# Two layers of decomposed-position attention: low-rank factors and key places loaded behind x

## The chip, the cores and the metric

The kernel runs on one core of one Trainium2 chip. The metric is the device time of one execution in microseconds (us); lower is better. The core's engines each work through an instruction stream of their own: TensorE (PE, with its weight loads shown as PEld), VectorE (DVE), ScalarE (ACT), GpSimd (POOL) and SyncE (SP). Transfers that SP issues run on the queue that the profile calls q1, those that POOL issues on q0; both are carried out by the same 16 DMA engines.

## The reference

x has 48 x 48 positions of 768 channels. Two layers follow each other, each adding attention of its normalised input to that input. Cut to what matters:

```python
def _gn(v, G=32, eps=1e-5):            # 32 groups of 24 channels, over all positions
    m, s = mean(v by group), var(v by group)
    return (v - m) / sqrt(s + eps)

# layer 0, low-rank addition to q and v
qkv = x @ qkv_w + qkv_b
u = x @ FacTu_w                        # 768 -> 16
qkv[..., :C]  += u @ q_facts_w @ FacTv_w
qkv[..., 2*C:] += u @ v_facts_w @ FacTv_w
# both layers, 12 heads of 64
attn = softmax((q * scale) @ k.T + rel_h + rel_w)   # rel_h, rel_w from q and tables
out = attn @ v @ proj_w + proj_b

x = x + layer0(_gn(x))
x = x + layer1(_gn(x))
```

## The kernel before

All of x fits on the chip. It is handled in six blocks of 384 tokens (`NQB`, `QB`). Layer 0 begins with `load_transposed`: SP issues the six loads of x (1152 KB each), then the first third of the weights of k (`weights.load(0)`, 768 KB, tile `w_k`). `weights.begin` then issues the small loads of layer 0. TensorE turns each block with 18 transposes into PSUM (tiles `psx`), ACT copies the result out (`raw`, six copies for a block), and DVE takes statistics of each copy (`stats`, L187).

`group_norm` follows. DVE aggregates the statistics (`mv`, L204), TensorE sums them over the channels of a group (`sum_mean`, L210) and spreads the mean back (`bc_mean`), then the same for the variance (`sum_var`, `bc_rstd`). With mean and deviation DVE normalises the blocks (L249), and the products of k begin (`ps_k`, L523), then those of v, then those of q; the seven products of a two-by-two block scheme replace eight. Attention, the output projection and layer 1 come after that.

The low-rank part of layer 0 is not computed on x. `fold` adds FacTu @ facts @ FacTv to the weights of v and q, when those are read, with products of the tiles `low` and `fv`. To make `low`, the generator `low_rank` turns FacTu (tile `fu`) with six TensorE transposes (`psu`), DVE copies them (`fuT`, two copies), and four products with the small matrices (tile `facts`, made wider by three POOL copies, L321) give `psl`, which ACT copies into `low`. The generator stops before its first product; each `next` on it runs it on to the next stop. Two of its products stand before `sum_mean` on TensorE, the others between the steps of `group_norm`.

Three other things stand on POOL at the start. It builds two one-hot tables, stores them (`f_hot`, L143) and loads them back four times as `places` (L154), which the scores of attention read. `weights.spread` copies the position tables from `flat` into `tab` (L311, four copies), which the products of q's positions read. And it stores the six raw blocks as residuals (`f_res`, L192, 1152 KB each), which the output projection of layer 0 reads.

Each engine runs its own stream in the order in which a scheduler set it when the kernel was built; `in_order` marks instructions for that scheduler. [...] The scheduler's order of the kernel before is, on POOL: f_hot, fu, f_hot, four fv and two facts loads, places, the facts copies, the table copies, the six f_res stores. On SP: x, `w_k`, bt, v_bias, four flat loads, the second third of `w_k`.

A second copy of the whole computation stands in the program under a branch for results that fail a test of range (`shifted`); it isn't executed here.

Of the kernel before, what the change touches and what calls it, by code (L numbers as in the profile page):

```python
# [18 lines left out]
P = 128  # L19
# [15 lines left out]
RANK = 16  # L35
# [36 lines left out]
def compute(ctx: ExitStack, tc: tile.TileContext, x, layers, out, run, bad):  # L72


    nc = tc.nc
    shifted = bad is None
# [53 lines left out]
    with ExitStack() as hots:  # L130
# [4 lines left out]
        for i, (rows, pattern, shape) in enumerate(parts):  # L135
            t = hotp.tile([rows, *shape], F32, tag=f"h{i}", name=f"hot_{i}")
# [15 lines left out]
    def load_places():  # L152
        for i in range(4):
            nc.gpsimd.dma_start(  # L154
                places[ts(i, 2 * KG)].bitcast(F32), hot.rearrange("k (u n) -> k u n", u=2)
            )

    def in_order(instruction):

        tc.keep_in_program_order(instruction)  # L160
# [4 lines left out]
    def load_transposed(xT, raw, res, weights, low_rank):  # L165


        with tc.tile_pool(name="ps_x", bufs=3, space=PSUM) as ps_x:
            loaded = [xT[b].rearrange("p t q -> p (t q)") for b in range(NQB)]
            loaded = [l.rearrange("p (j c) -> p j c", j=TPB) for l in loaded]  # L170
            for b in range(NQB):
                nc.sync.dma_start(loaded[b], x[ts(b, QB), :].rearrange("(j p) c -> p j c", p=P))
            weights.load(0)
            weights.begin()
            if not shifted:
                load_places()
            for b in range(NQB):
                if b == 2:
                    next(low_rank)
                for t in range(CT):  # L180
                    ps = ps_x.tile([P, QB], F32, tag="ps", name=f"psx_{b}_{t}")
                    for j in range(TPB):
                        in_order(nc.tensor.transpose(
                            ps[:, ts(j, P)], loaded[b][:, j, ts(t, P)], ident
                        ))
                    nc.scalar.copy(raw[b][:, t, :], ps)
                    nc.vector.bn_stats(stats[:, t, b, :], raw[b][:, t, :])  # L187

            weights.spread()
            for b in range(HB):  # L190
                for i in (b, b + HB):
                    in_order(nc.gpsimd.dma_start(res[i], raw[i]))  # L192
# [63 lines left out]
    class Weights:  # L256
# [20 lines left out]
        def begin(self):  # L277
            one, ly = self.one, self.ly
            if ly.lora is not None:
                u_w, q_f, v_f, o_w = ly.lora  # L280
                self.fu = one.tile([P, CT, RANK], F32, tag="fu", name="fu")
                nc.gpsimd.dma_start(self.fu, u_w.rearrange("(t p) r -> p t r", p=P))
                self.facts = one.tile([RANK, 2, P], F32, tag="facts", name="facts")
                nc.gpsimd.memset(self.facts, 0.0)
                self.out = one.tile([P, C], F32, tag="fv", name="fv")
                self.low = one.tile([P, 2, C], F32, tag="low", name="low")
                for i, f in enumerate((q_f, v_f)):
                    nc.gpsimd.dma_start(self.facts[:, i, 0:RANK], f)
                for r in range(4):
                    nc.gpsimd.dma_start(self.out[r * 32 : r * 32 + RANK, :], o_w)  # L290
            self.bt = one.tile([P, 3 * CT], F32, tag="bt", name="bt")
            nc.sync.dma_start(self.bt, ly.qkv_bt)
            nc.sync.dma_start(v_bias[self.li], ly.qkv_bt[:, 2 * CT :])

            self.tables = []
            for a, src in enumerate((ly.relh_t, ly.relw_t)):
                flat = one.tile([P, REL], F32, tag=f"flat{a}", name=f"flat{a}")
                tab = one.tile([P, REL, 2], F32, tag=f"tab{a}", name=f"tab{a}")  # L300
                nc.gpsimd.memset(tab, 0.0)
                for par in range(2):
                    nc.sync.dma_start(flat[ts(par, HD), :], src)
                self.tables.append((flat, tab))
# [954 lines left out]

    es = ExitStack()  # L1260
    xT, gn, weights = begin(0, es)
    for li, ly in enumerate(layers):
        last = li == len(layers) - 1
        with tc.tile_pool(name="p1_kv", bufs=1, **REUSE) as kv:
            raw = xT
            low_rank = weights.low_rank(kv)
            if li == 0:


                raw = [  # L1270
                    kv.tile([P, 2, CT, QB], F32, tag=tag, name=f"raw_{tag}")
                    for tag in ("t1", "t2", "vw")
                ]
                raw = [raw[b % HB][:, b // HB] for b in range(NQB)]
                load_transposed(xT, raw, residuals[0], weights, low_rank)
                first, k_steps = third_of_k(weights, 0)
            normalise = group_norm(xT, raw, gn, low_rank, k_steps)
            qd, kd, vd, rel_d = project(ly, li, xT, kv, weights, first, normalise)
# [5 lines left out]
        with tc.tile_pool(name="p3_w", bufs=1, **REUSE) as p3:  # L1284
# [22 lines left out]
            if last:  # L1307
                p3_first = es.enter_context(
                    tc.tile_pool(name="p3_first", bufs=1, side="right", **REUSE)
                )  # L1310

                y_2, y_1, *first_out, y_0 = (
                    p3_first.tile(shape, F32, tag=name, name=name)
                    for name, shape in (
                        ("y_1_2", [P, 2, C]), ("y_1_1", [P, 2, C]), ("oT_1_0", [P, CT, QB]),
                        ("oT_1_1", [P, CT, QB]), ("y_1_0", [P, 2, C]),
                    )
                )
                first_out += [y_0, y_1, y_2]
            else:  # L1320
                xT, gn, weights = begin(1, es)
                first_out = [xT[HB], xT[NQB - 1]]
# [73 lines left out]
```

## Time and profile before

| | us |
|---|---|
| median of 3 runs | 3257.7 (3254.74 to 3259.03) |
| profiled execution, its own time | 3255.04 |
| its span, first to last instruction | 3253.3 |
| TensorE busy | 3204.2 (98%) |
| first transpose of block 0 | 6.28 |
| first transpose of block 5 | 24.32 |
| group sums of the mean (sum_mean) | 29.14 |
| first product of k | 36.37 |
| first scores of attention | about 507 |

The profile is one execution; its times count from the first instruction of the span. In the timeline a row has the start and the length of a run of equal instructions, the engine, the line, the operation with its tiles, the count, and in brackets how long the engine stood idle before and what ended that. The length of a DMA row is the time its issue took at the issuer, not that of the transfer.

### The profile page before, as it was taken

Reading aid. Unit: us, or ns where it says so; the run is one execution under the profiler, and the core shown is the slowest. Engines: PE = TensorE matmul, PEld = TensorE weight load, DVE = VectorE, ACT = ScalarE, POOL = GpSimd, SP = SyncE. Lnnn points to the kernel's source line nnn. Section 1 sums busy time; section 2 is a strip of 40 time slices with the busy share of each in tenths; the row PEclk is TensorE's granted clock in tenths of the full one; section 3 lists DMA queues with packets and bytes.
Section 4 is the critical chain, followed back from the end, with each engine's and each line's share of the span. In section 5 each row is a group of like instructions: output and inputs, shape, how many; then the busy total and the mean of one; then the engine's idle time right before and its main releaser. Section 6 shows DMA issues by size and latency. Waiting matters only on the chain.

```text
span 3253.3 us, 50008 instructions
## 1 busy us (share of the span) xinstructions
PE 3204.2 (98%) x19600; PEld 1990.3 (61%) x19600; DVE 2112.3 (65%) x2281; ACT 1450.7 (45%) x1673; POOL 470.1 (14%) x855
## 2 busy tenths in 40 slices
PE   8999999999999999999989999999999999999999
PEld 5555666665666565666555566666566565656565
DVE  8532437777777777777775234577777777777764
ACT  3111436555555565553012024556556566555520
POOL 2145110000000000000012541102202221100000
PEclk9999999999999999999999999999999999999999
DMA  7333388353526263634234335765636473735351
GB/s 264 130 88 74 128 257 219 84 127 79 138 68 153 64 156 65 142 75 151 112 117 141 68 100 183 244 151 135 124 109 156 106 167 81 164 76 132 70 203 60
DMA packets 225155, 419.76 MB, mean 129 GB/s; under 512 B 43616, under 2 KB 111104, under 8 KB 221072
## 3 DMA queue, kind: packets, MB, share of 16 engines
q1 hardware_dynamic: 177712, 255.35, 31.9%
q0 software_dynamic: 47200, 161.12, 16.3%
q8 instruction: 158, 2.59, 0.3%
q14 instruction: 85, 0.70, 0.1%
HBM read 260.35 MB, written 155.97 MB: 128 GB/s over the span
## 4 chain that ended last, share of the span: by engine, by line
PE 81%; issue 12%; POOL 2%; DMA 2%; DVE 1%; SPq 1%; ACT 1%; POOLq 0%; DVEq 0%; ACTq 0%
PE ps_sc L954 34%; PE ps_ov L954 25%; PE ps_v L523 7%; PE ps_q L698 4%; PE ps_k L523 4%; PE psy L1186 4%; PE ps_d L954 1%; PE psr L637 1%; DMA f_r<-relw 1%; POOL f_k L567 1%; POOL f_q L630 1%; DMA flat<-in_relh_t_dram 0%; POOL f_r L663 0%; PE psc L637 0%; ACT pt L981 0%
## 5 line engine op out<-in xcount | busy, mean ns | idle before, releaser
L987 DVE TENSOR_TENSOR sum<-sum,pt 128x1024 f32<-128x1024 f32 (+1 forms) x960 | 1071.1, 1116 | 185.7 <-ACT pt L981 95.5
L981 ACT ACTIVATE pt<-ps_sc 128x1024 f32<-128x1024 f32 (+1 forms) x1080 | 1010.4, 941 | 168.9 <-PE ps_sc L954 84.0
L954 PE MATMUL ps_sc<-q,k 64*128 64x512 f32 (+1 forms) x8640 | 1082.2, 370 | 1.6 <-DVE relw L392 0.7
L954 PEld LDWEIGHTS ps_sc<-q,k 64*128 64x128 f32 x8640 | 778.9, 185 | 213.8 <-issue 45.6
L954 PE MATMUL ps_ov<-pt,v 128*64 128x512 f32 (+1 forms) x4320 | 857.7, 551 | 0.0
L954 PEld LDWEIGHTS ps_ov<-pt,v 128*64 128x64 f32 x4320 | 301.1, 137 | 497.6 <-issue 443.0
L954 PE MATMUL ps_sc<-rel,places 64*128 64x512 f32 (+1 forms) x2160 | 411.9, 370 | 1.4 <-DMA rel<-f_r 1.4
L698 PE MATMUL ps_q<-xT,w_q 128*128 128x384 f32 x864 | 285.3, 488 | 0.7 <-DVE v L587 0.7
L1032 POOL DMA_DIRECT2D f_rec<-rec x120 | 58.8, 494 | 1570.6 <-DVE rec L1021 1569.0
L1026 ACT ACTIVATE o<-o,v_bias 128x512 f32<-128x512 f32 (+1 forms) x60 | 40.9, 682 | 451.4 <-DVE o L1025 451.4
L698 PEld LDWEIGHTS ps_q<-xT,w_q 128*128 128x128 f32 x864 | 163.1, 191 | 110.3 <-issue 2.6
L954 PEld LDWEIGHTS ps_sc<-rel,places 64*128 64x128 f32 x2160 | 210.4, 185 | 32.8 <-issue 2.2
L1021 DVE RECIPROCAL rec<-ps_d 128x512 f32<-128x512 f32 (+1 forms) x60 | 181.9, 3031 | 2.5 <-PE ps_d L954 2.5
L601 POOL DMA_DIRECT2D f_v<-v x288 | 137.9, 488 | 105.8 <-DVE v L587 100.9
L987 DVE TENSOR_TENSOR sum<-pt 128x1024 f32<-128x1024 f32 (+1 forms) x60 | 67.0, 1116 | 124.3 <-ACT pt L981 124.3
L704 DVE TENSOR_SCALAR x_q<-ps_q,bt 128x384 f32<-128x384 f32 x72 | 44.3, 617 | 158.8 <-PE ps_q L698 158.8
L523 PE MATMUL ps_k<-xt,w_k 128*128 128x384 f32 x432 | 143.4, 487 | 3.6 <-DVE xt L427 2.6
L996 ACT CAST sum<-sum 128x1024 bf16<-128x1024 f32 (+1 forms) x60 | 57.7, 961 | 168.4 <-DVE sum L987 168.4
L523 PE MATMUL ps_k<-xT,w_k 128*128 128x384 f32 x324 | 115.4, 510 | 4.7 <-DVE xT L249 4.6
L523 PEld LDWEIGHTS ps_k<-xt,w_k 128*128 128x128 f32 x432 | 81.5, 190 | 63.0 <-PE ps_k L523 3.0
L999 DVE TENSOR_TENSOR sum<-sum,sum 128x1024 bf16<-128x1024 f32 (+1 forms) x60 | 67.1, 1119 | 61.6 <-ACT sum L998 61.6
L997 DVE TENSOR_TENSOR sum<-sum,sum 128x1024 f32<-128x1024 f32 (+1 forms) x60 | 67.1, 1119 | 61.6 <-ACT sum L996 61.6
(183 smaller groups left out, 2474.0 us busy)
## 6 DMA issues: line engine op xcount, KB each, us to landing
rel<-f_r SPq DMA_DIRECT2D x1152, 96.0 KB, 4.3
f_k<-xs POOLq DMA_DIRECT2D x72, 384.0 KB, 2.9
f_q<-xs_q POOLq DMA_DIRECT2D x48, 576.0 KB, 3.8
k<-f_k SPq DMA_DIRECT2D x48, 576.0 KB, 4.9
q<-f_q SPq DMA_DIRECT2D x96, 256.0 KB, 3.4
f_r<-relh POOLq DMA_DIRECT2D x48, 432.0 KB, 5.0
f_r<-relw POOLq DMA_DIRECT2D x8, 2592.0 KB, 18.1
f_v<-v POOLq DMA_DIRECT2D x288, 48.0 KB, 2.0
```

What stands on the lines that cost most here:

```text
L523: nc.tensor.matmul(ps, lhsT=x, rhs=y, start=(t == 0), stop=(t == HP - 1))
L601: nc.gpsimd.dma_start(vd[to : to + KG, :], v[ts(r, KG), k])
L698: nc.tensor.matmul(ps, lhsT=w[:, t, ts(pr, P)], rhs=xT[b][:, t, :], start=(t == 0), stop=(t == CT - 1),)
L954: in_order(nc.tensor.matmul(*args, **kwargs))
L981: nc.scalar.activation(pt, ps[:, :, 0 : self.n], AF.Exp)
L987: nc.vector.tensor_add(self.sum, self.first if kt == 1 else self.sum, pt)
L996: nc.scalar.copy(hi, self.sum)
L997: nc.vector.tensor_sub(self.sum, self.sum, hi)
L999: nc.vector.tensor_sub(lo, self.sum, mid)
L1021: nc.vector.reciprocal(self.rec, ps)
L1032: nc.gpsimd.dma_start(recs[li][2 * self.pair + r : 2 * self.pair + r + 1, to], self.rec[r * HD : r * HD + 1, :],)
L1186: nc.tensor.matmul(ps, lhsT=x, rhs=y, start=(t == 0), stop=(t == HP - 1))
```

## The change

Four lines of order change. The loads of `fu`, `facts` and `fv` are issued by SP, behind x and `w_k`, where POOL issued them. `load_places` moves from before the blocks to behind `weights.spread()`. The first step of the generator `low_rank` (FacTu's transposes, their copies and the widening of `facts`) is called behind the last block of x, where it was called between blocks 1 and 2.

```diff
             weights.begin()
-            if not shifted:
-                load_places()
             for b in range(NQB):
-                if b == 2:
-                    next(low_rank)
                 for t in range(CT):
...
                     nc.vector.bn_stats(stats[:, t, b, :], raw[b][:, t, :])
+            next(low_rank)
 
             weights.spread()
+            if not shifted:
+                load_places()
             for b in range(HB):
                 for i in (b, b + HB):
                     in_order(nc.gpsimd.dma_start(res[i], raw[i]))
...
-                nc.gpsimd.dma_start(self.fu, u_w.rearrange("(t p) r -> p t r", p=P))
+                nc.sync.dma_start(self.fu, u_w.rearrange("(t p) r -> p t r", p=P))
...
-                    nc.gpsimd.dma_start(self.facts[:, i, 0:RANK], f)
+                    nc.sync.dma_start(self.facts[:, i, 0:RANK], f)
                 for r in range(4):
-                    nc.gpsimd.dma_start(self.out[r * 32 : r * 32 + RANK, :], o_w)
+                    nc.sync.dma_start(self.out[r * 32 : r * 32 + RANK, :], o_w)
```

## The prediction

> **What bounds the kernel now.** I read the page first, then the stretches and the timeline of the first 60 us, then the DMA queues. The page:
>
> ```profile
> span 3253.3 us, 50008 instructions
> PE 3204.2 (98%) x19600; PEld 1990.3 (61%) x19600; DVE 2112.3 (65%) x2281; ACT 1450.7 (45%) x1673; POOL 470.1 (14%) x855
> ```
>
> TensorE is busy nearly throughout, and what the change moves is done long before anything behind the first product of k reads it. So the change is worth what it does to the time at which that product starts, 36.37 us. The stretches before it (columns: length, busy time and count of each engine, granted clock, DMA share, GB/s):
>
> ```profile
> 9.50:16.00 6.50, 5.28 (x43) 4.21 (x42) 6.04 (x14) 4.51 (x13) 3.23 (x10) 1.00 1.05 295
> 20.00:24.00 4.00, 2.56 (x20) 1.90 (x18) 3.25 (x8) 2.79 (x8) 0.00 (x0) 1.00 1.04 395
> 30.00:36.00 6.00, 5.59 (x22) 3.74 (x22) 2.86 (x12) 1.21 (x3) 2.25 (x5) 0.50 0.99 393
> ```
>
> No engine is full; the DMA is, and from 9.5 to 16 us it moves only 295 GB/s, against 395 later and 415 from 5 to 6.2 us. That dip is when the small POOL loads (fu, facts, fv) and the end of hot's store run. The timeline (start, duration, engine, line, operation):
>
> ```profile
> 12.82 1.99 POOL L154 DMA_DIRECT2D places<-f_hot  x4 [2.58 <-DMA f_hot<-hot]
> 21.37 2.40 PE L183 MATMUL psx<-ident,xT 128*128 128x128 f32 x18 [1.21 <-DMA xT<-in_x_dram]
> 24.32 2.40 PE L183 MATMUL psx<-ident,xT 128*128 128x128 f32 x18 [0.56 <-ACT raw_t L186]
> 27.84 1.24 POOL L311 COPY tab<-flat 64x95 f32<-64x95 f32 x4 [12.54 <-DMA flat<-in_relh_t_dram]
> 28.17 1.18 DVE L204 BATCH_NORM_AGGREGATE mv<-stats 128x2 f32<-128x36 f32 x6
> 29.02 2.18 POOL L192 DMA_DIRECT2D f_res<-raw_t  x4
> 29.14 0.46 PE L210 MATMUL sum_mean<-mv,gin 128*16 128x2 f32 x6 [0.94 <-ACT low L341]
> 36.37 7.95 PE L523 MATMUL ps_k<-xT,w_k 128*128 128x384 f32 x18 [0.77 <-DVE xT L249]
> ```
>
> Blocks of x arrive slower than TensorE turns them (2.40 us for one); the last starts at 24.32 (its wait is put down to ACT, but ACT had kept pace, so it was x's landing), its statistics end at 28.25, the group sums start at 29.14. One line matters most: POOL waits 12.54 us for flat before its table copies, and only behind those does it issue the six stores of raw x (f_res, 1152 KB each). That wait keeps 7 MB of stores away from x.
>
> **The change, part by part.** In the built order of the changed kernel POOL has: hot's stores, the four places loads, f_res 0, 3, 1, 4, the facts copies, f_res 2, one table copy, f_res 5, three table copies. f_res 0 waits only for ACT's first six copies (block 0), f_res 3 for block 3, f_res 1 for nothing more, f_res 4 for block 4. The facts copies wait for facts' DMAs, now on SP behind x, w_k and fu. On TensorE the six fu transposes wait for fu and stand before the sums; on DVE the two fuT copies stand before the aggregates. So the sums wait for fu, and fu is last in a ring that competes with four stores.
>
> Step 1, when the stores start. POOL loses seven issues (0.89 + 2x0.49 + 0.49 + 1.44 = 3.8 us) and issues hot's second store about 0.6 us sooner. It landed 12.82 - 6.15 = 6.7 us after issue; so places go at about 11 to 12 us, and f_res 0 behind their 1.99 us at 13 to 14. Under a full x queue places took 5.4 us to land, so the first store packets move by 17 to 18 us. Until then x runs at the 395 to 415 GB/s of its undisturbed rows instead of 295: blocks 0 to 3 and most of 4 are in by 17.5, so f_res 3 and 1 are released near 18, f_res 4 at 21 to 23. All four have begun before x and w_k are in.
>
> Step 2, how the two queues share the engines. A late stretch of this trace, 424 to 427 us, has loads of 4.6 KB packets on q1 against larger stores on q0:
>
> ```profile
> q0 software_dynamic: 61, 0.72, 84.1%
> q1 hardware_dynamic: 64, 0.28, 22.4%
> ```
>
> Packet for packet (61 to 64), not byte for byte (0.72 MB to 0.28). A packet of x is 3 KB, of w_k 1 KB, of f_res 9 KB (6.99 MB in the 838 packets of 30 to 47 us, 80 of them tiny). So x keeps about a quarter while a store runs, w_k about a tenth. [...] If the engines shared by time instead, w_k would end near 27 us and the sum below would come to +3.
>
> Step 3, when fu lands. Everything on q0 up to f_res 4 then goes ahead of the end of w_k, and fu is behind w_k, so only bytes count: x 7.08 MB, w_k 0.79, places 0.13, four stores 4.72, together 12.72 MB. At 405 GB/s (395 for x, 411 for the stores from 30 to 47 us) this is 31.4 us from 2.4 us on, when the queue is full; plus 1.0 us tail (block 0 would be in at 2.4 + 2.9 = 5.3 and TensorE starts at 6.28). fu lands at 34.8. At 415 GB/s it is 34.0; if mixed reads and writes only reach the 325 GB/s that x averaged (7.08 MB from 2.4 to 24.2), the 6.7 MB after 17.5 us take 20.6 instead of 16.5 us: 38.9.
>
> Step 4, from fu to the sums. Warm: transposes 0.82, last fuT copy 0.5, aggregates 1.18 on DVE while TensorE does two low-rank products (1.55 warm): sums 2.8 us after fu. At the half clock, which the third stretch shows at 0.50: transposes doubled to 1.6, two products at 1.62 each (the row at 31.08 has one at that price): 5.0. TensorE would have stood idle for some microseconds before fu, and it was halved at 30 us even in the kernel before; I take 3.9, a little over half way. The facts copies (0.50 on POOL after landing) fit inside. The sums start at 38.7 instead of 29.14: +9.6.
>
> Step 5, the rest. From the sums to the first k product the order is unchanged, and already runs at half clock: 0. w_k lands before fu and is first read behind the group mean: 0. DVE from 50 to 80 us is full (10.0, 10.0 and 9.5 of each 10 us) and does the same work, but one xs part (1.02) and two w_k sums (2x0.56) now precede the second block's sums, up to 1.1 us later for TensorE's wait at 60.19: I take +0.4, between 0 and 1.1. f_res 2 and 5 leave after facts and table, about 36 and 40 us, and end by 46 to 48 with the second w_k beside them; the first f_k store comes 10 us after 51.76, the second w_k is read after 65: 0, and if that cover of over 13 us were gone, POOL's f_k would wait for them in the queue. fv is read at the fold, beyond 120 us; bt with xs at 50.5 before: 0. [...]
>
> Sum: 9.6 + 0.4 = +10.0. The profiled execution took 3255.04 (span 3253.3), so 3265.0; the median of the runs is 2.7 above that execution: 3267.7.
>
> **Rivals.** (a) Not slower: the stores reach the engines only after x and w_k, say because the issue is late behind a full queue. For it: places took 5.4 us to land for 32 KB each. Then x and places end at 2.4 + 7.21/0.405 = 20.2, w_k 22.2, fu lands at 23.3; but DVE needs 36 statistics at 0.48 from 7.7 on, to 24.9; two fuT copies (0.99), the aggregates (1.18), the sums starting 0.2 before their end as they did: 26.9, -2.2, 3255.5. It decides when f_res 0 moves its first packets after about 22 us; against it, that would need 8 us from issue. The least the change can come to is this case with the clock kept full, where the two later low-rank products save some 0.8 each: -3.8. (b) Part: f_res 1 and 4 get behind w_k (sharing by time, or a late block 4): two stores of 2.9 us less, +4.2, 3261.9. (c) Worse: mixed rates as above, +4.1 on top, +14.1, 3271.8. That x simply is hidden anyway (same start of the sums) has no place: they wait for fu by order.
>
> **How the numbers follow.** About 0.2% (6.5 us) is what a measurement of this kernel can tell from no change. Main case (+6.5 to +12): 0.58; (c) 0.14; (b) 0.12; (a) 0.16. Slower is main and (c): 0.72; same is (a) and (b) less 0.02: 0.26; faster 0.02. The range leaves out (a) and the far end: from just under (b), 3259.0, to a little over (c), 3273.5.
>
> **What would show it.** Right: f_res issues at 13 to 23 us, x's last two blocks 3 us and more apart, fu's transposes at about 35 us, the sums at 38 to 39, the first k product near 46, and from there the same spacing as before. Step 1 is wrong if the last block of x starts before 24; step 2 if w_k's landing comes before f_res 4's; step 4 if the transposes come near 35 and the sums not within 5 us. The whole is wrong if the sums start before 29.

## The result, and the profile after

| | before | after |
|---|---|---|
| median, us (lowest to highest) | 3255.32 (3252.22 to 3259.03, 6 runs) | 3269.68 (3267.23 to 3271.58, 6 runs) |
| profiled execution, its own time | 3255.04 | 3269.19 |
| its span | 3253.3 | 3267.2 |

The ratio is 1.0043, with a 95% interval of 1.0033 to 1.0053: slower by 14.0 us (10.7 to 17.3). The prediction had 3267.7 us, in a range from 3259.0 to 3273.5. Its sum for the difference was +10.0 us; the time came closer than that because the kernel before has a median of 3255.32 over six runs, where the prediction started from 3257.7. In the changed kernel the line numbers from the loop over the blocks on are one to four lower than in the kernel before.

The head of the page after. TensorE's busy time has grown by 6.7 us, though its work is the same: products at half clock count as longer (block 5's 18 transposes took 4.07 us at a granted clock of 0.50, and 2.40 in the kernel before at 1.00).

```profile
span 3267.2 us, 50010 instructions
...
PE 3210.9 (98%) x19600; PEld 1994.7 (61%) x19600; DVE 2113.2 (65%) x2281; ACT 1451.1 (44%) x1673; POOL 467.7 (14%) x848
```

The stretches after (same columns as before: length, busy time and count of PE, PEld, DVE, ACT and POOL, granted clock, DMA share, GB/s):

```profile
9.50:16.00 6.50, 6.50 (x48) 5.60 (x47) 6.18 (x14) 6.02 (x16) 2.55 (x5) 1.00 1.04 391
20.00:24.00 4.00, 2.47 (x12) 2.50 (x13) 0.97 (x2) 1.24 (x3) 0.00 (x0) 0.68 0.99 410
30.00:36.00 6.00, 4.07 (x18) 3.70 (x18) 3.36 (x6) 4.06 (x7) 0.00 (x0) 0.50 0.93 323
36.00:40.00 4.00, 3.41 (x9) 1.81 (x10) 2.19 (x8) 0.60 (x3) 1.51 (x6) 0.50 0.43 159
```

Two things are to be seen. The dip that the small POOL loads made is gone: 391 GB/s from 9.5 to 16 us, where it was 295. And from 20 to 24 us the DMA engines are as full as before (410 GB/s, where it was 395), but TensorE gets little to do (busy for 2.47 of the 4.00 us), and its granted clock is 0.68 there and 0.50 from 30 to 40 us. The bytes that move there are others. The timeline names them:

```profile
10.93 1.98 POOL L154 DMA_DIRECT2D places<-f_hot  x4 [4.31 <-DMA f_hot<-hot]
...
12.90 0.57 POOL L191 DMA_DIRECT2D f_res<-raw_t  x1
...
18.43 1.07 POOL L191 DMA_DIRECT2D f_res<-raw_t  x2 [4.96 <-ACT raw_t L182]
...
21.53 3.76 PE L179 MATMUL psx<-ident,xT 128*128 128x128 f32 x18 [3.94 <-DMA xT<-in_x_dram]
...
26.15 0.53 POOL L191 DMA_DIRECT2D f_res<-raw_t  x1 [6.65 <-ACT raw_t L182]
...
30.20 4.07 PE L179 MATMUL psx<-ident,xT 128*128 128x128 f32 x18 [4.91 <-DMA xT<-in_x_dram]
...
36.55 1.45 PE L327 MATMUL psu<-ident,fu 128*16 128x128 f32 x6 [2.27 <-DMA fu<-in_FacTu_w_dram]
...
37.01 0.50 POOL L320 COPY facts<-facts 16x32 f32<-16x32 f32 x3 [10.32 <-DMA facts<-in_v_facts_w_dram]
...
38.51 1.18 DVE L203 BATCH_NORM_AGGREGATE mv<-stats 128x2 f32<-128x36 f32 x6
...
40.87 0.32 PE L209 MATMUL sum_mean<-mv,gin 128*16 128x2 f32 x6
...
48.02 2.29 PE L522 MATMUL ps_k<-xT,w_k 128*128 128x384 f32 x3 [0.77 <-DVE xT L248]
```

Four stores of raw x are issued from 12.90 us on, where the first was at 29.02. The blocks of x that remain come 8.7 us apart (21.53 and 30.20; before 21.37 and 24.32). FacTu is there at 36.55, the sums start at 40.87 instead of 29.14 and the first product of k at 48.02 instead of 36.37: 11.65 us of the 13.9 us by which the span grew are lost there.

### The profile page after: what moved, and what is told of

Its sections match the earlier page's. It is cut to its first block, busy times and chain, and to the rows that moved or that the text cites. A ratio compares the mean times of both kernels' runs of the same rounds, so it can differ in the third digit from the quotient of the medians.

```text
span 3267.2 us, 50010 instructions
## 1 busy us (share of the span) xinstructions
PE 3210.9 (98%) x19600; PEld 1994.7 (61%) x19600; DVE 2113.2 (65%) x2281; ACT 1451.1 (44%) x1673; POOL 467.7 (14%) x848
## 4 chain that ended last, share of the span: by engine, by line
PE 78%; issue 14%; DMA 3%; POOL 2%; DVE 1%; SPq 1%; ACT 0%; POOLq 0%; DVEq 0%; ACTq 0%
PE ps_sc L953 34%; PE ps_ov L953 25%; PE ps_v L522 7%; PE ps_k L522 4%; PE psy L1185 4%; PE ps_q L697 2%; PE ps_d L953 1%; DMA f_r<-relw 1%; DMA w_k<-in_qkv_w_dram 1%; POOL f_q L629 1%; POOL f_r L662 1%; POOL f_k L566 1%; DMA flat<-in_relh_t_dram 0%; PE psr L636 0%; DMA rel<-f_r 0%
## 5 line engine op out<-in xcount | busy, mean ns | idle before, releaser
L953 PEld LDWEIGHTS ps_sc<-rel,places 64*128 64x128 f32 x2160 | 210.3, 185 | 33.3 <-DMA rel<-f_r 2.0
```

Source lines behind the costliest of these rows:

```text
L953: in_order(nc.tensor.matmul(*args, **kwargs))
```

## The experiments

Each ran beside the kernel before on the same chip. The table has the times from the profile of each (us) and the ratio to the kernel before. In the kernel before, the wait on `flat` stands ahead of all six stores on POOL. In after and e5 it stands ahead of the last store alone, in e2 ahead of the last three, and in e6 ahead of none of the halves on POOL.

| | last block of x | fu's transposes | group sums | first k product | ratio [95%] |
|---|---|---|---|---|---|
| before | 24.32 | 12.14 | 29.14 | 36.37 | 1 |
| after | 30.20 | 36.55 | 40.87 | 48.02 | 1.0043 [1.0033, 1.0053] |
| e1, places early | 21.93 | 24.62 | 27.86 | 33.81 | 0.9999 [0.999, 1.0008] |
| e2, only places late | 31.39 | 12.87 | 37.34 | 44.26 | 1.0031 [1.0019, 1.0043] |
| e3, only low-rank late | 24.10 | 26.34 | 30.03 | 35.99 | 1.0002 [0.9992, 1.0011] |
| e4, stores on SP | 21.76 | 24.62 | 27.69 | 34.83 | 0.9992 [0.9983, 1.0002] |
| e5, short store rows | 25.80 | 36.80 | 41.11 | 48.26 | 1.0045 [1.0029, 1.006] |
| e6, half the stores | 25.09 | 31.63 | 35.95 | 43.10 | 1.0029 [1.0018, 1.004] |
| e7, e4 and fuT on ACT | 21.95 | 24.78 | 27.70 | 34.85 | 0.9994 [0.9985, 1.0003] |

**e1: places back in their old place.** Against the changed kernel; everything else of the change stays.

```diff
             weights.begin()
+            if not shifted:
+                load_places()
             for b in range(NQB):
...
             weights.spread()
-            if not shifted:
-                load_places()
```

> The changed kernel with load_places back in its old place, all else as changed (fu, facts, fv on SP behind x and w_k, first low-rank step behind the last block). On POOL the stores of raw x then stand behind the table copies again. Theory 1 (the stores that were let go early took the DMA engines from x, w_k and fu): x's last block starts near 21 us, fu's transposes near 24, the sums near 27, the time 2 us under the kernel before (0 to -4). Theory 2 (fu behind w_k in SP's ring and the low-rank work ahead of the sums cost by themselves): sums still at 37 us or later, the time 10 to 14 us over the kernel before.

The loads of places are issued at the same time as in the changed kernel (11.06 and 10.93 us); what differs is the order behind them on POOL. The timeline of e1:

```profile
11.06 1.98 POOL L154 DMA_DIRECT2D places<-f_hot  x4 [4.46 <-DMA f_hot<-hot]
...
24.62 0.82 PE L328 MATMUL psu<-ident,fu 128*16 128x128 f32 x6 [0.29 <-DMA fu<-in_FacTu_w_dram]
...
25.18 0.49 POOL L321 COPY facts<-facts 16x32 f32<-16x32 f32 x3 [12.14 <-DMA facts<-in_v_facts_w_dram]
...
27.86 0.30 PE L210 MATMUL sum_mean<-mv,gin 128*16 128x2 f32 x6
...
28.22 1.36 POOL L311 COPY tab<-flat 64x95 f32<-64x95 f32 x3 [2.55 <-DMA flat<-in_relh_t_dram]
...
30.57 2.15 POOL L192 DMA_DIRECT2D f_res<-raw_t  x4
```

The scheduler now puts the facts copies and the table copies ahead of the stores, and the stores go at 30.57 us. The sums start 1.3 us before those of the kernel before, with fu still behind `w_k`, and the time is that of the kernel before. So the whole loss hangs on the place of the stores; that fu waits in SP's ring (its transfers in the order in which it issues them) behind x and `w_k` costs nothing that the time shows.

**e2: only places moved.** Against the kernel before:

```diff
             weights.begin()
-            if not shifted:
-                load_places()
...
             weights.spread()
+            if not shifted:
+                load_places()
```

> The kernel before with load_places moved behind the table copies' place in the text, nothing else changed. On POOL three stores (0, 3, 1) then stand ahead of the table copies. Theory 1: all three run beside x's last two blocks; the last block starts near 30 to 32 us, the sums at 35 to 38, the time 6 to 9 us over the kernel before. Theory 2: fu is early and POOL's, so the sums stay at 29 and the time within 1 us of the kernel before.

```profile
16.67 0.59 POOL L192 DMA_DIRECT2D f_res<-raw_t  x1
...
20.91 1.07 POOL L192 DMA_DIRECT2D f_res<-raw_t  x2 [3.65 <-ACT raw_t L184]
...
31.39 3.95 PE L181 MATMUL psx<-ident,xT 128*128 128x128 f32 x18 [7.57 <-DMA xT<-in_x_dram]
...
36.36 1.23 POOL L311 COPY tab<-flat 64x95 f32<-64x95 f32 x4 [14.38 <-DMA flat<-in_relh_t_dram]
```

Moving those four small loads is enough: three stores go ahead of the wait on flat, the last block of x waits 7.57 us, and the time is +10 us. The expected +6 to +9 was missed a little. The first k product is 7.9 us late, inside the expected +6 to +9, but at 85 us TensorE waits another 2.64 us for DVE's `xt`, and a stretch at a lower clock follows (granted clock 0.83 on average from 84 to 94 us; the 24 products from 85.33 on took 9.70 us, where 24 took 7.90 from 52.37 on); behind it the products are 11.0 us late. Why the wait falls there, and not in the changed kernel, was not settled.

**e3: only the low-rank step late.** Against the kernel before, with fu, facts and fv still on POOL:

```diff
             for b in range(NQB):
-                if b == 2:
-                    next(low_rank)
...
+            next(low_rank)
```

> The kernel before with only the first low-rank step moved behind the last block. Stores held as before. Theory 1: nothing queues for the DMA; DVE's two fuT copies (1.0 us) now stand between the statistics and the aggregates, TensorE's transposes (0.8) behind block 5: 0 to +2 us, sums at 29 to 31. Theory 2 with the low-rank work as the part that costs: +4 us or more.

The sums start 0.9 us later than before (30.03), the first k product 0.4 us earlier, and the time is the same. So six transposes and two copies between the statistics and the aggregates are no loss when fu is there.

**e4: the stores moved to SP.** Against the changed kernel:

```diff
             for b in range(HB):
                 for i in (b, b + HB):
-                    in_order(nc.gpsimd.dma_start(res[i], raw[i]))
+                    in_order(nc.sync.dma_start(res[i], raw[i]))
```

> The changed kernel with the six stores of raw x issued by SP, behind x, w_k, fu and flat in one ring, so that they can't overtake; load_places stays late. Theory 1: sums near 27 us as in the first experiment, time 0 to 4 us under the kernel before; the second third of w_k lands behind the stores near 44 us, ahead of its use. Theory 2: sums at 37 us or later, time 10 to 14 us over the kernel before.

```profile
21.76 2.40 PE L179 MATMUL psx<-ident,xT 128*128 128x128 f32 x18 [0.52 <-DMA xT<-in_x_dram]
...
24.62 0.82 PE L327 MATMUL psu<-ident,fu 128*16 128x128 f32 x6 [0.47 <-DMA fu<-in_FacTu_w_dram]
...
27.69 0.32 PE L209 MATMUL sum_mean<-mv,gin 128*16 128x2 f32 x6
...
28.15 3.27 SPq L191 DMA_DIRECT2D f_res<-raw_t  x4
```

With places late and the low-rank step late, as in the changed kernel, but the stores behind x, `w_k`, fu and flat in SP's order, the loss is gone. This is the second way to the same end as e1: it is the stores, not the place of places or of the low-rank step.

**e5: the same stores in shorter rows.** Against the changed kernel; the output projection reads the scratch back with the same rearrangement:

```diff
-                    in_order(nc.gpsimd.dma_start(res[i], raw[i]))
+                    in_order(nc.gpsimd.dma_start(res[i].rearrange("t p q -> p t q"), raw[i]))
...
-                        nc.sync.dma_start(y[i], res[pair[i]])
+                        nc.sync.dma_start(y[i], res[pair[i]].rearrange("t p q -> p t q"))
...
-    residuals = [[scratch(f"res{li}_{b}", [P, CT, QB]) for b in range(NQB)] for li in range(2)]
+    residuals = [
+        [scratch(f"res0_{b}", [CT, P, QB]) for b in range(NQB)],
+        [scratch(f"res1_{b}", [P, CT, QB]) for b in range(NQB)],
+    ]
```

> The changed kernel with one thing different: layer 0's residual scratch is laid out by channel tile, so a store of a raw block (the same 1152 KB, the same issue on POOL, the same place in the order) is written in rows of 1.5 KB where it was written in rows of 9 KB. Turns of packets (each queue moves one packet in its turn, whatever its size): x's 3 KB packets now weigh two of the stores', so x keeps about two thirds while a store runs; its last block starts at 22 to 24 us (30.20 in the changed kernel), w_k and fu get ahead of part of the stores, fu's transposes at 28 to 33 us (36.55), the sums 4.3 us behind them, the time +3 to +9 us over the kernel before. If rows are joined to packets of 4.6 KB: 25 to 27 and 33 to 36. Sharing by bytes or by time, or four stores that go first whatever their shape: block 5 at 30, fu at 36 to 37, +13 us as in the changed kernel. Small rows that are slow by themselves: block 5 early, but the DMA rate from 20 to 30 us well below 405 GB/s and fu no earlier than 36.

The rows were joined, so the case of 4.6 KB packets holds. The DMA queues of the changed kernel from 24 to 28 us (packets, MB, share of the engines), then those of e5 in the same stretch:

```profile
q0 software_dynamic: 157, 1.30, 76.8%
q1 hardware_dynamic: 156, 0.43, 26.9%
```

```profile
q0 software_dynamic: 299, 1.30, 79.6%
q1 hardware_dynamic: 299, 0.33, 23.0%
```

In both, the two queues move the same number of packets, whatever their size: 157 to 156, and 299 to 299. A store packet is 8.3 KB on average in the first, 4.3 KB in the second (MB by packets). So in these stretches the queues shared the engines packet for packet; whether they alternated by single packets of the profile or by several, the rows can't tell. The last block of x comes at 25.80 instead of 30.20, as expected (25 to 27). But fu comes at 36.80, a little beyond the expected 33 to 36, and nothing is gained at the end. The smaller packets changed whose bytes came first, but fu, behind x and `w_k` in its ring, still came when all the bytes of the four stores had moved: the two queues had moved 4.88 and 8.11 MB by 36.6 us in e5, and 4.88 and 8.11 MB by 36.4 us in the changed kernel.

**e6: half of each store.** Against the changed kernel:

```diff
-                    in_order(nc.gpsimd.dma_start(res[i], raw[i]))
+                    in_order(nc.gpsimd.dma_start(res[i][:, 0:HP], raw[i][:, 0:HP]))
+                    in_order(nc.sync.dma_start(res[i][:, HP:], raw[i][:, HP:]))
```

> The changed kernel with each store of a raw block cut in two: channel tiles 0 to 2 stay on POOL where they were, tiles 3 to 5 are issued by SP behind the loads of the position tables. So half of the bytes can go ahead of w_k and fu. If only the bytes ahead of fu count (step 3 of the prediction, with the tail of 2.7 us that the changed kernel showed): x 7.08, w_k 0.79, places 0.13 and five or six half stores of 0.59 MB are 10.9 to 11.5 MB; at 405 GB/s from 2.4 us on, and the tail, fu's transposes stand at 32.0 to 33.6 us (36.55 in the changed kernel), the sums at 36 to 38 (40.87), and the time is +7 to +10 us over the kernel before, where the changed kernel was +14. If the loss were one of the stores being there at all, whatever their bytes (a queue that takes turns badly, reads and writes mixed): 36 to 37, 41 and +13 to +14.

```profile
20.43 3.65 PE L179 MATMUL psx<-ident,xT 128*128 128x128 f32 x18 [2.60 <-DMA xT<-in_x_dram]
...
23.91 0.53 POOL L191 DMA_DIRECT2D f_res<-raw_vw  x1
...
25.09 2.40 PE L179 MATMUL psx<-ident,xT 128*128 128x128 f32 x18 [1.02 <-DMA xT<-in_x_dram]
...
31.63 1.45 PE L328 MATMUL psu<-ident,fu 128*16 128x128 f32 x6 [4.13 <-DMA fu<-in_FacTu_w_dram]
...
35.95 0.32 PE L210 MATMUL sum_mean<-mv,gin 128*16 128x2 f32 x6
```

By 31.4 us the stores' queue had moved 3.23 MB, against 4.88 MB that it moved ahead of fu in the changed kernel. The 1.65 MB less are 4.1 us at 405 GB/s; fu came 4.92 us earlier and the sums as much. The time is +9.4 us (5.9 to 13.0), where +7 to +10 was expected of bytes and +13 to +14 of a loss that doesn't go by bytes. fu and the sums are just before the expected stretches.

**e7: stores on SP, and fuT's copies on ACT.** Against e4:

```diff
-                nc.vector.tensor_copy(fuT[:, cols], ps[0:RANK])
+                nc.scalar.copy(fuT[:, cols], ps[0:RANK])
```

> The version that the runs so far point to: the changed kernel with the six stores of raw x issued by SP behind the position tables (as in the run before), and FacTu's two transposed copies moved from DVE, where they stand ahead of the aggregates, to ACT. x, w_k and fu go undisturbed, so block 5 at 21.8 and fu's transposes at 24.6 us as there; the aggregates start up to 1.0 us earlier and the sums at 26.9 to 27.5 (27.69 there, 29.14 before). If the start of the first k product passes through to the end: 2 to 3.5 us faster than before (0.06 to 0.1%), about at the limit of what five rounds tell. If an extra half-clock stretch later takes it back, as in one profile so far: no difference.

```profile
25.48 0.50 POOL L320 COPY facts<-facts 16x32 f32<-16x32 f32 x3 [12.29 <-DMA facts<-in_v_facts_w_dram]
...
25.80 1.18 DVE L203 BATCH_NORM_AGGREGATE mv<-stats 128x2 f32<-128x36 f32 x6
...
26.03 1.75 PE L337 MATMUL psl<-fuT,facts 16*128 16x384 f32 x4 [0.42 <-POOL facts L320]
...
27.70 0.32 PE L209 MATMUL sum_mean<-mv,gin 128*16 128x2 f32 x6
```

The aggregates did start 0.7 us earlier than in e4 (25.80 against 26.53), but the sums didn't (27.70 against 27.69): the low-rank products stand before them, and those wait for the facts copies on POOL, whose last load lands at about 25.4 us. This expectation was missed, and neither e4 nor e7 is faster than the kernel before by what its intervals can tell.

## Why the prediction was right, point by point

**The mechanism** held: stores of raw x overtake x, `w_k` and fu once POOL's wait on flat no longer holds them, and the sums wait for fu. e1 and e4 took away the stores' early start alone, in two ways, and the loss went; e2 made that early start alone, and most of the loss came.

**Step 1** (places at 11 to 12, f_res 0 at 13 to 14, f_res 3 and 1 near 18) was right within 0.5 us: 10.93, 12.90, 18.43. f_res 4 came at 26.15, not at 21 to 23, because block 4 of x was itself held back (21.53) and its transposes ran at half clock (granted clock 0.50 from 22 to 24 us; 3.76 us, not 2.40). It made no difference: that store was still ahead of the end of `w_k`.

**Step 2** (packet for packet) is shown by the rows of 24 to 28 us (157 packets to 156) and by those of e5 (299 to 299). It does not hold of every stretch: from 21 to 22 us, between two stores, q0 moved 9 packets and q1 123, and in e5 from 20 to 24 us q0 moved 185 and q1 288. The sign that the prediction set for this step came out too: f_res 4 landed at 35.8 us (9.6 us from its issue), `w_k` at 36.4 (29.7 us from its issue).

**Step 3** had its main term right and its tail (the time from the end of that sum to fu's transposes) wrong. The trace of the changed kernel, from the start to 34 us:

```profile
DMA packets 3998, 12.72 MB, mean 374 GB/s; under 512 B 363, under 2 KB 1117, under 8 KB 3485
```

That is the predicted 12.72 MB, at 34.0 us for the predicted 33.8; by 36.4 us 13.01 MB had moved, as the sum had left out FacTu and the four fv loads (0.25 MB together). But fu's transposes came 2.7 us after 33.8, not 1.0. The tail had been read from the first block of x, in 3 KB packets; the end of this one is shown by the stretch from 33 to 37 us:

```profile
DMA packets 1254, 0.64 MB, mean 160 GB/s; under 512 B 944, under 2 KB 1174, under 8 KB 1238
```

944 of its 1254 packets are under 512 B (FacTu alone is 768 rows of 64 bytes), and the rate is 160 GB/s, not 405. Two stretches inside it (the last two columns are DMA share and GB/s):

```profile
34.00:35.00 1.00, 0.28 (x2) 0.00 (x0) 0.84 (x3) 0.82 (x3) 0.00 (x0) 0.50 1.13 234
35.00:36.00 1.00, 0.00 (x0) 0.00 (x0) 0.39 (x1) 1.00 (x1) 0.00 (x0) 0.50 0.26 45
```

From 34 to 35 us the engines are full but move 234 GB/s; from 35 to 36 us they are a quarter busy, and less after that (a share of 0.03 from 36 to 37). The 0.29 MB that moved from 34 to 37 us would be 0.7 us at 405 GB/s (an estimate), so more of the tail passes with engines nearly idle than with full engines on small packets. Why the last packets come so unevenly stays open. The stores are not what makes the tail: in e1 and e4, where none runs beside x, the working of rival (a) ends `w_k` at 22.2 us, and fu's transposes stand at 24.62, 2.4 us later. In e6 the sum with a tail of 2.7 came out 0.4 us too late at least, so the tail is no constant.

**Step 4**: from fu to the sums 4.32 us, taken at 3.9 between 2.8 and 5.0. All of it ran at half clock (granted clock 0.50 from 36 to 40 us; the transposes 1.45 us, where the warm price was 0.82), so the place a little over half way was too low by 0.4. Tail and chain together are the 2.2 us by which the sums miss (40.87 against 38.7). In the changed kernel the clock was low behind the waits of 3.94 and 4.91 us ahead of blocks 4 and 5 (1.00 from 20 to 21 us and 0.50 from 22 to 24; 1.00 from 26 to 28 and 0.56 from 28 to 30), stayed at 0.50 through the work with gaps from 36.55 us on, and came back at about 52.1, 4.1 us after the unbroken work began at 48.02. Shorter waits had a low clock behind them too. In e6 the granted clock was 0.79 on average from 20 to 28 us, and the transposes behind a wait of 2.60 us took 3.65 us. In the kernel before it was 0.50 from 30 to 36 us, though TensorE had had no wait longer than 1.22 us since 14 us. So these runs show no length of wait that is a safe one.

**Step 5**: the first k product came +11.65 (sums +11.73), so the order between them cost nothing, as said. The first product of v was at 186.56, +12.10 to the 174.46 before: +0.45 since the first k product, where the step had taken +0.4 for DVE's changed order. The second `w_k` load and the late stores cost nothing there. What the step had not foreseen is the rest: +0.6 up to the end of layer 0, and +1.3 near 1700 us, where the profiled execution of the changed kernel has a stretch at half clock (granted clock 0.50 from 1691 to 1693 us, 0.86 on average from 1688 to 1700) that the kernel before hasn't (1.00 from 1680 to 1700). e1 has one at the same place (0.86 on average too), e6 a weaker one (0.91 on average from 1685 to 1705 us), e7 none (1.00). The work of layer 1 is the same in all. With one profile of each, whether the stretch belongs to a kernel or to an execution stays open.

**The rivals.** (a), stores only behind x and `w_k`, is what e4 is in all but name: the sums at 27.69, where that rival's working had 26.9 (it had fu at 23.3, and fu's transposes stand at 24.62), and 34.83 at the first k product. Of its -2.2 us the profile of e4 has -1.5 there and -1.7 at the end, too few for the runs to tell: 0.9992, 0.9983 to 1.0002. (b), part of the stores, is e6, where the cost went by bytes. (c), slow mixed traffic, was wrong: the DMA moved 410 GB/s from 20 to 24 us and 433 from 24 to 28, with reads and writes mixed. That the total came near (c)'s +14.1 is not its mechanism: the tail, the half clock and the later losses made it up.

**Where the gain went.** Taking the small loads off POOL's queue did bring x in earlier: 391 to 394 GB/s from 9.5 to 16 us in the changed kernel and in e1, the last block 2.4 us earlier in e1. But in e1 the start of the first k product was only 2.55 us earlier, of 3255, and the stretch at a lower clock near 1700 us took most of it back in its profile (-3.75 us ahead of layer 1, -0.28 at the end).

## What to carry to other kernels

Before moving a load on a queue, ask which later instruction of that queue now comes free: here a wait for an unrelated small load had been holding 7 MB of stores back, and the order that a scheduler makes can lose it by a move of four 32 KB loads. Stores that nobody needs soon belong behind the loads that the critical path waits for, by order or on the same queue, not by luck. Here fu, behind x and `w_k` in its ring, waited for the bytes of both queues, so count bytes; with store packets of 8 KB or of 4 KB that wait was nearly the same (fu's transposes at 36.55 and 36.80 us).

## What the runs showed of the hardware that I had not expected

An issue can hold SP for long: issuing fu took SP 9.61 us and the second 1 KB of facts 11.46 us in the changed kernel, the first 1 KB of facts 0.54:

```profile
9.43 9.61 SPq L281 DMA_DIRECT2D fu<-in_FacTu_w_dram  x1
...
19.15 0.54 SPq L287 DMA_DIRECT2D facts<-in_q_facts_w_dram  x1
...
19.73 11.46 SPq L287 DMA_DIRECT2D facts<-in_v_facts_w_dram  x1
...
31.24 2.08 SPq L289 DMA_DIRECT2D fv<-in_FacTv_w_dram  x4
```

It is not the change that brings such issues: in the kernel before, the issue of bt behind `w_k` took 7.96 us. In e4, where the stores come only later, fu took 5.95 us to issue, and the same facts and fv loads are through by 22 us instead of 33.3. In the changed kernel the last long one ends at 31.19, about when x's last block is in (30.20), but in e5 at 29.66, where that block is in at 25.80; so it is not simply the landing of x that ends it. What holds the issuer, no run isolates. What stands behind such an issue is issued after it: in the changed kernel fv at 31.24 us, bt at 36.35 (behind a wait of 3.0 us for `w_k` to land), flat at 37.22 and the second part of `w_k` at 40.78; in this kernel that had cover.
